# First-layer rows copied unscaled out of PSUM by ScalarE, leaky in SBUF by VectorE, six buffers for them, and a later schedule behind

## The chip, the cores and the metric

The kernel runs on one core of one Trainium2 chip. The metric is the device time of that core in microseconds, the median of several runs. The core has five engines, each with its own queue of instructions taken in order: TensorE (PE in the profile, its weight loads PEld), VectorE (DVE), ScalarE (ACT), GpSimd (POOL) and SyncE (SP, which issues most DMAs). They wait for one another by semaphores.

## The reference

A graph layer: 12500 nodes with 128 features, 412500 edges with 64 features, sorted by destination. For each edge, query, key and edge products go through a two-layer network with leaky ReLU (slope 0.2). Eight scores per edge are averaged, a softmax runs over all edges, and weighted value rows are summed per source node. Then come two normalisations.

```python
attn_in = jnp.concatenate([q[src], k[tgt], eh], axis=-1)
hmid = jax.nn.leaky_relu(attn_in @ A1 + b1, SLOPE)
scores = jax.nn.leaky_relu(hmid @ A2 + b2, SLOPE)
w = jax.nn.softmax(scores.mean(axis=-1), axis=0)
out = jax.ops.segment_sum(w[:, None] * v[tgt], src, num_segments=num_nodes)
y = h + out
```

`y` is normalised with `gamma` and `beta`, added to `x`, and normalised again.

## The kernel before

Two pipelines run side by side, each written as a generator or a list of steps, and interleaved in program order.

The first makes records. Edges come in 403 groups of 1024. For each group TensorE gathers key and value rows with one-hot matrices and adds the edge product (`rows`, L940 and L947) into banks of PSUM. ScalarE copies the banks to SBUF records (`evacuate`, L958 and L959; five buffers `rec`). GpSimd scatters every record to a table in HBM, sorted by block of source nodes (L970, 3224 indirect DMAs). VectorE works out the places (`onehots` L860 to L880, `masked` L910, `places` L921 and L923). A group takes six steps.

The second, `sums_of`, reads the table back in 250 units of up to 16 tiles of 128 rows (10 rounds of 25 units; units of two rounds have 12 tiles). A unit passes through these functions:

- `load` (L1154): one DMA into a buffer `rt`, six of which there are (two more in the last round). `sources` (L1199, L1201), `turned` and `put` (L1212, L1217), `spread` (L1222) and `load_q` (L1180) bring the source numbers and the queries to the partitions that need them; `onehot` (L1232) makes one-hot matrices of them.
- `hidden` (L1244, L1254): four times in a unit, four tiles each. TensorE adds the transposed key part and the query part in a bank of PSUM.
- `sloped` (L1265): ScalarE writes 0.2 times the bank into a buffer `hm` in SBUF. `leaky` (L1269): VectorE takes the maximum of bank and `hm`, back into `hm`.
- `scores` (L1280), `above_zero` (L1294), `heads` (L1306): the second layer, summed over heads.
- `maxima` (L1316, L1321): VectorE's score `S` and its maximum `mx` per partition; `maximum` (L1327): TensorE transposes `mx`; `reference` (L1336, L1337): VectorE's running reference `ref`; `weights` (L1346): ScalarE's exponentials `w`.
- `select` (L1355) and `weigh` (L1369): one-hot matrices of the nodes, times the weights. `add` (L1402): TensorE sums value rows. `before_it` (L1379) loads the sums of the round before into `old`, `lowered` (L1388, L1391) rescales, `total` (L1419, L1412) adds them, `store` (L1431) writes them.

Banks of PSUM come from one ring of five, `bank()`, which `rows`, `hidden` and `scores` share, so a new product waits until the bank of five before has been read. The buffers `hm` come from the pool `hp`, which has five.

What sets the order is the table that `lags` returns (L1109): for each function, how many steps behind the unit's own step `s0` it is issued. A new unit begins every 8 steps. `hidden` of piece k stands at `s0 + 2k`, and `onehot`, `sloped` and `leaky` count from there. A step's functions are issued in the order in which they were entered, those with `late=1` behind the others. A load stands no sooner than one step behind the last `add` of the unit that had its buffer (`load_at = mine[-held] + 1`), and at `s0 - 19` in all rounds but the last.

`closing` ends the kernel: it adds `beta` to `x` into a table (`rows_x`, `moved`, `put_x`), and then normalises 14 groups of seven blocks. It takes its buffers from pools opened late, in the space of the record pipeline.

Of the kernel before, what the change touches and what calls it, by code (L numbers as in the profile page):

```python
# [10 lines left out]
FP = mybir.dt.float32  # L11
# [4 lines left out]
AF = mybir.ActivationFunctionType  # L16
ALU = mybir.AluOpType
# [4 lines left out]
P = 128  # L22
D = 128
# [3 lines left out]
SLOPE = 0.2  # L27
NB = 7
# [3 lines left out]
MORE = 2  # L32
# [13 lines left out]
WR = 257  # L46
# [432 lines left out]
def sorted_path(  # L479
# [8 lines left out]
    nc = tc.nc  # L488
# [34 lines left out]
    for j, part in enumerate((1.0, -1.0)):  # L523
        nc.vector.tensor_scalar(
            A2s[:, H + 1 + j : H + 2 + j], A2s[:, H : H + 1], part * SLOPE / (1 - SLOPE), None,
            op0=ALU.mult,
# [6 lines left out]
    for j, part in enumerate((1.0, -1.0)):  # L533
        nc.vector.tensor_scalar(
            b2_r[:, H + 1 + j : H + 2 + j], b2_r[:, H : H + 1], part * SLOPE / (1 - SLOPE), None,
            op0=ALU.mult,
# [10 lines left out]
        out=signs, in_=signs, compare_op=ALU.not_equal, fill=SLOPE - 1, base=-(H + 2),  # L547
# [40 lines left out]
    TB = max(t for *_, t in plan.rounds)  # L588
    work = ctx.enter_context(ExitStack())
    pool = lambda name, bufs, **k: work.enter_context(tc.tile_pool(name=name, bufs=bufs, **k))  # L590
    hp = pool("hid", 5)
    Wqh, bias_qh, Wkv, bias_kv = (
        wts[:, 2 * D * i : 2 * D * (i + 1)].rearrange("k (s d) -> k s d", s=2)
        for wts in [hp.tile([D, 4 * P], FP, name="hm") for _ in range(2)] for i in range(2)
# [19 lines left out]
    with tc.tile_pool(name="prep", bufs=1) as prep, tc.tile_pool(  # L614
        name="pprep", bufs=1, space=PSUM
# [28 lines left out]
    blk = const.tile([P, T], BF)  # L644
# [79 lines left out]
    def spans():  # L724
# [21 lines left out]
    above = const.tile([P, P], BF)  # L746
    nc.gpsimd.memset(above, 1.0)
    nc.gpsimd.affine_select(
        out=above, in_=above, compare_op=ALU.is_gt, fill=0.0, base=0,
# [20 lines left out]
    late = {}  # L770
# [318 lines left out]
    for p, (*_, t) in enumerate(plan.rounds):  # L1089
        wide = max(1, min(BLK, WIDTH // t))  # L1090
# [11 lines left out]
    state = {}  # L1102
# [6 lines left out]
    def lags(p):  # L1109

        return dict(
            every=EVERY, lead=25 if p == NR - 1 else 19, sources=-13, turned=-12, spread=-7, q=-7,
            onehot=-2, sloped=2, leaky=3, scores=10, above=12, heads=13, maxima=15, maximum=15,
            reference=17, weights=18, old=13, lowered=21, select=16, weigh=18,
            add=(21, 22, 24, 25), total=27, store=30,
        )

    def sums_of(bp):


        plans, s0, free, starts, ends = [], 19, ([], []), {}, {}
        for p, bs, t in units:
            nt = len(bs) * t
            nk = -(-nt // 4)
            o = lags(p)
# [7 lines left out]
            s0 = max(s0, load_at + o["lead"] - 1)  # L1133
            if plans:
                s0 = max(s0, plans[-1][2] + EVERY)
# [9 lines left out]
        def do(step, fn, *args, late=0):  # L1145
            steps.setdefault(max(int(step // 1), 0), []).append((late + step % 1, fn, args))
# [113 lines left out]
            st["hm"][k] = hp.tile([D, 4 * P], FP, name="hm")  # L1260
            st["ph", k] = ph

        def sloped(i, t0, c, n, k):
            hm = state[i]["hm"][k][:, : n * P]
            nc.scalar.activation(hm, state[i]["ph", k][:, : n * P], AF.Copy, scale=SLOPE)  # L1265

        def leaky(i, t0, c, n, k):
            hm, ph = state[i]["hm"][k][:, : n * P], state[i].pop(("ph", k))
            nc.vector.tensor_tensor(hm, ph[:, : n * P], hm, op=ALU.max)  # L1269


        def slices(m):
# [166 lines left out]
        for i, (nt, nk, s0, load_at, o) in enumerate(plans):  # L1439
            do(load_at, load, i)  # L1440
            do(s0 + o["sources"], sources, i)
            do(s0 + o["turned"], turned, i)
            do(s0 + o["turned"], put, i)
            do(s0 + o["spread"], spread, i)
            do(s0 + o["q"], load_q, i)
            for k, (c, c1) in enumerate(pieces(i)):
                n, s = c1 - c, s0 + 2 * k
                t = units[i][2]
                for u in range(-(-c // t), (c1 - 1) // t + 1):
                    do(s + o["onehot"], onehot, i, u)  # L1450
                do(s, hidden, i, c, c, n, k)
                do(s + o["sloped"], sloped, i, c, c, n, k, late=1)
                do(s + o["leaky"], leaky, i, c, c, n, k, late=1)
            do(s0 + o["scores"], scores, i, 0, nt)
            do(s0 + o["above"], above_zero, i)
            do(s0 + o["heads"], heads, i, 0, nt)
            do(s0 + o["maxima"], maxima, i)
            do(s0 + o["maximum"], maximum, i, late=1)
            do(s0 + o["reference"], reference, i)
            do(s0 + o["weights"], weights, i)  # L1460
            do(s0 + o["old"], before_it, i)
            do(s0 + o["lowered"], lowered, i)
            for j, t0 in enumerate(range(0, nt, 4)):
                n = min(4, nt - t0)
                if t0 % SEL == 0:
                    m = min(SEL, nt - t0)
                    do(s0 + o["select"] + 2 * j, select, i, t0, m)
                do(s0 + o["weigh"] + 2 * j, weigh, i, t0, n)
                do(s0 + o["add"][j], add, i, t0, n)
            do(s0 + o["total"], total, i)  # L1470
            do(s0 + o["store"], store, i)
# [8 lines left out]
    def closing(bp, do, s0, s1, s2):  # L1480

        gb = {}

        def wide(b):
            return b.rearrange("p (o d) -> p o d", o=1).to_broadcast([P, NB, D])

        def three(b, k):
            return b[:, k * NB * D : (k + 1) * NB * D].rearrange("p (b d) -> p b d", d=D)

        def rows_x(g):  # L1490
            gb["x", g] = t = late["end"].tile([P, 2, 2, WR], FP, name="rec")
            t = t.rearrange("p a b w -> p (a b w)")
            nc.sync.dma_start(out=three(t, 0), in_=x[:, g * NB : (g + 1) * NB, :])
            nc.sync.dma_start(out=t[:, NB * D : NB * D + D], in_=beta.to_broadcast([P, D]))

        def moved(g):
            t = gb["x", g].rearrange("p a b w -> p (a b w)")
            nc.gpsimd.tensor_add(three(t, 0), three(t, 0), wide(t[:, NB * D : NB * D + D]))

        def put_x(g):  # L1500
            t = gb.pop(("x", g)).rearrange("p a b w -> p (a b w)")
            nc.sync.dma_start(out=xtab[:, g * NB : (g + 1) * NB, :], in_=three(t, 0))

        def load_gamma():
            gb["gamma"] = late["gamma"].tile([P, D], FP, name="gamma")
            nc.sync.dma_start(out=gb["gamma"], in_=gamma.to_broadcast([P, D]))

        for g in range(ng):
            do(s0 + 24 + 12 * g, rows_x, g)
            do(s0 + 30 + 12 * g, moved, g)  # L1510
            do(s0 + 34 + 12 * g, put_x, g)
        do(s0 + 30, load_gamma)


        def factors():
# [68 lines left out]
            st["y", k] = [parts[j // 4][:, j % 4 * D : (j % 4 + 1) * D] for j in range(NB)]  # L1584

        def diagonals(st):
            t = late["end"].tile([P, 2, 2, WR], FP, name="rec").rearrange("p a b w -> p (a b w)")
            st["dg"] = three(t, 0)
            nc.gpsimd.tensor_mul(
                st["dg"], wide(ident),  # L1590
                gb["facs"][:, st["bl"]].rearrange("p (b o) -> p b o", o=1)
                .to_broadcast([P, NB, D]),
            )
# [228 lines left out]
    with tc.manual_schedule():  # L1822
        n1, n3 = 6 * plan.rounds[0][1], 6 * G
        n0 = n1 * 9 // 10
        i1 = 6 * min(plan.gate, plan.rounds[0][1]) - 12
        pieces = list(fill(2))
        fills = [(i1 * j // len(pieces), piece) for j, piece in enumerate(pieces)]
        fills = sorted(fills, key=lambda piece: piece[0])[::-1]
        tabs, made, nt = tables(), 0, 1 + (2 * ng - 1) * (10 + 6) + ng
        more, sent, ne = later(), 0, 11 * (len(chunks) - 1)  # L1830
        done, r = 0, 0
        for i, _ in enumerate(_ for p in range(NP) for _ in make(p)):
            while fills and fills[-1][0] <= i:
                fill_piece(*fills.pop()[1])
            while made < nt and made * n0 < i * nt:
                next(tabs, None)
                made += 1
            while sent < ne and sent * n0 < i * ne:
                next(more, None)
                sent += 1  # L1840
            if i == n1:
                for _ in tabs:
                    pass
                for _ in more:
                    pass
                spans()
                covered()
                tab_pool.close()
                steps, starts = sums_of(pool("blk", BLKS))
            if i < n1:  # L1850
                continue
            while r + 1 < NR and i >= 6 * begun[r + 1]:
                r += 1
            if r + 1 < NR:
                until = starts[r] + (starts[r + 1] - starts[r]) * (i - 6 * begun[r]) / (
                    6 * (begun[r + 1] - begun[r])
                )
                while done < until:
                    for fn, args in steps[done]:
                        fn(*args)  # L1860
                    done += 1
        while done < starts[-1]:
            for fn, args in steps[done]:
                fn(*args)
            done += 1
        making.close()
        for name, of, bufs, k in (
            ("blk", "blk2", MORE, {}), ("end", "end", 4, {}), ("gamma", "gam", 1, {}),
            ("psm", "psm2", 1, dict(space=PSUM)),
        ):  # L1870
            late[name] = far(of, bufs, **k)
        for step in steps[done:]:
            for fn, args in step:
                fn(*args)
# [73 lines left out]
```

## Time and profile before

| | |
|---|---|
| runs | 5765.57 us median of 3, 5764.45 to 5776.47 |
| the profiled execution | 5754.63 us, its span 5752.9 us |
| mean granted TensorE clock | 0.833 |
| leaky, L1269 | 932 instructions, 631.7 us busy |
| scaled copy, L1265 | 932 instructions, 547.7 us busy |

The profile's page counts the busy time of each engine over the span and shows the span in 40 slices. Its groups of instructions give the line, the engine, the operation, its output and input by the program's names, the count, then the busy time in us and the mean of one in ns, and last the idle time of the engine just before them with what ended it. A wait is put down to the instruction that came last by the profile; "remote" stands for a releaser on none of the core's engines, "issue" for none that the profile shows. All durations are those of one execution.

### The profile page before, as it was taken

The numbers are of one execution on the slowest core, as the hardware profiler recorded it, in microseconds if no ns is written. First come the engines' busy times: TensorE is split into PE (matmuls) and PEld (weight loads), VectorE is DVE, ScalarE is ACT, GpSimd is POOL, SyncE is SP. The second block draws the span as 40 slices with busy tenths as digits, with TensorE's granted clock in tenths as the row PEclk, the third lists the DMA queues.
The fourth block names the chain that finished last, engine by engine and source line by source line (L and its number), as shares of the span: only waits on it lengthen the run. The fifth ranks groups of instructions, "written<-read, shape, count | busy, mean of one in ns | idle before, by whom it ended". The sixth has DMA issues, their size and how long they took to land. (4 is left out here: it accounts for less than half of the span.)

```text
span 5752.9 us, 91349 instructions
## 1 busy us (share of the span) xinstructions
PE 4343.1 (75%) x29928; PEld 3185.9 (55%) x29928; DVE 4003.1 (70%) x8452; ACT 3093.0 (54%) x8846; POOL 3315.0 (58%) x3279
## 2 busy tenths in 40 slices
PE   4546536777777877778778888887787888888887
PEld 2334324555555656555556655566665555556677
DVE  7778745666667677666666777767776766676677
ACT  2432224445555666555555665556555565556776
POOL 4776666666566655566665656555555556665103
PEclk7667657788888898888888898898888888888999
DMA  6888766766778888778788888888888887877975
GB/s 195 265 258 270 249 202 220 229 224 223 240 272 269 268 278 275 257 251 270 257 265 274 276 270 284 278 263 261 274 268 268 271 269 259 269 272 255 330 282 185
DMA packets 728991, 1487.94 MB, mean 259 GB/s; under 512 B 157584, under 2 KB 328227, under 8 KB 726710
## 3 DMA queue, kind: packets, MB, share of 16 engines
q1 hardware_dynamic: 537410, 1056.51, 57.7%
q0 software_dynamic: 154752, 424.43, 20.0%
q10 hardware_dynamic: 36340, 1.05, 0.4%
q8 instruction: 237, 3.88, 0.3%
q14 instruction: 252, 2.06, 0.1%
HBM read 902.30 MB, written 579.32 MB: 258 GB/s over the span
## 5 line engine op out<-in xcount | busy, mean ns | idle before, releaser
L970 POOL DMA_INDIRECT rtab<-rec,idx x3224 | 3230.3, 1002 | 2067.6 <-issue 830.3
L958 ACT ACTIVATE rec<-bank 128x512 f32<-128x512 f32 x1612 | 879.9, 595 | 1489.0 <-remote 653.1
L1402 PE MATMUL psm<-rt,ohw 128*128 128x128 f32 x7448 | 1226.2, 310 | 128.8 <-issue 126.1
L1369 ACT ACTIVATE ohw<-ohs,w 128x128 f32<-128x128 bf16 x3724 | 1214.2, 401 | 32.7 <-remote 8.5
L1402 PEld LDWEIGHTS psm<-rt,ohw 128*128 128x128 f32 x7448 | 1086.9, 218 | 214.0 <-issue 165.2
L1269 DVE TENSOR_TENSOR hm<-bank,hm 128x512 f32<-128x512 f32 x932 | 631.7, 678 | 390.2 <-ACT hm L1265 253.2
L940 PE MATMUL bank<-kvs,ohd 128*128 128x256 bf16 x3224 | 607.2, 309 | 366.7 <-ACT rec L958 255.8
L1244 PE MATMUL bank<-ident,rt 128*128 128x128 f32 x3724 | 681.2, 309 | 237.2 <-ACT z L1294 81.7
L1265 ACT ACTIVATE hm<-bank 128x512 f32<-128x512 f32 x932 | 547.7, 588 | 571.1 <-remote 214.6
L1244 PEld LDWEIGHTS bank<-ident,rt 128*128 128x128 f32 x3724 | 481.5, 158 | 524.2 <-issue 275.7
L947 PE MATMUL bank<-WeS,eat 64*128 64x128 f32 x6448 | 715.7, 340 | 48.3 <-issue 47.0
L947 PEld LDWEIGHTS bank<-WeS,eat 64*128 64x128 f32 x6448 | 524.6, 221 | 273.2 <-issue 269.7
L910 DVE TENSOR_TENSOR ats<-pc,oh 128x792 f32<-128x792 f32 x403 | 393.2, 976 | 389.6 <-remote 172.3
L1254 PE MATMUL bank<-ohT,qs 128*128 128x512 bf16 (+3 forms) x2156 | 639.8, 391 | 30.6 <-issue 29.3
L940 PEld LDWEIGHTS <-ohd 128*128 128x128 bf16 x3224 | 343.4, 112 | 573.0 <-issue 473.1
L1232 DVE TENSOR_SCALAR ohT<-rowB,iotaP,power 128x512 bf16<-128x512 uint8 (+1 forms) x980 | 563.9, 580 | 77.7 <-DMA rowB<-row 38.2
L880 DVE TENSOR_SCALAR ohd<-dstb,node 128x1152 bf16<-128x1152 uint8 x404 | 566.0, 1401 | 33.2 <-remote 25.2
L1355 DVE TENSOR_TENSOR ohs<-iotaE,sl 128x512 bf16<-128x512 bf16 x932 | 395.5, 424 | 3.2 <-ACT ohw L1369 2.8
L921 DVE TENSOR_REDUCE pos<-ats 128x8 f32<-128x792 f32 x403 | 390.5, 969 | 2.5
L1280 PE MATMUL bank<-hm,A2s 128*32 128x512 f32 x1864 | 353.6, 660 | 29.9 <-issue 25.4
L1419 DVE SCALAR_TENSOR_TENSOR old<-old,by,psm 128x512 f32<-128x512 f32 (+1 forms) x225 | 164.6, 732 | 215.2 <-remote 73.4
L1306 PEld LDWEIGHTS psS<-headsum,z 128*128 128x128 f32 (+2 forms) x2000 | 277.2, 212 | 30.9 <-issue 25.7
(199 smaller groups left out, 3815.1 us busy)
## 6 DMA issues: line engine op xcount, KB each, us to landing
rt<-rtab SPq DMA_DIRECT2D x192, 2056.0 KB
eat<-in_ea SPq DMA_DIRECT2D x201, 512.0 KB
rt<-rtab SPq DMA_DIRECT2D x48, 1542.0 KB
qs<-qtab SPq DMA_DIRECT2D x240, 256.0 KB
atab<-old SPq DMA_DIRECT2D x240, 256.0 KB
old<-atab SPq DMA_DIRECT2D x216, 256.0 KB
rtab<-rec,idx POOLq DMA_INDIRECT x3224
dstb<-dtab SPq DMA_DIRECT2D x201, 256.0 KB
```

The source lines that it names most:

```text
L880: nc.vector.tensor_scalar(to, row[:, cols], node, None, op0=ALU.is_equal)
L940: nc.tensor.matmul(pk[h][:, i, :], ohd[h * (GT // 2) + j + i], kvs, start=(i == 0), stop=False,)
L947: nc.tensor.matmul(pk[h][:, i, :D], eat[half, (j + i) * P : (j + i + 1) * P], WeS[half, :], start=False, stop=(i == 1),)
L958: nc.scalar.activation(rec[:, h, :, : 2 * D], pk[h], AF.Copy)
L970: one_tile = nc.gpsimd.indirect_dma_start(out=rtab[:, :], out_offset=bass.IndirectOffsetOnAxis(ap=idxs[g][:, t : t + 1], axis=0), in_=rec[ ...
L1232: nc.vector.tensor_scalar(st["oh"][u][:, : t * P].rearrange("p (t q e) -> p t q e", q=4, e=32), st["rowB"][:, : nt * P] .rearrange("p (q t ...
L1244: nc.tensor.matmul(ph[:, j * P : (j + 1) * P], st["rt"][:, t0 + j, :D], ident, is_transpose=True, start=(j == 0), stop=False,)
L1254: nc.tensor.matmul(ph[:, cols], st["qs"][:, u, s, :], st["oh"][u][:, (j0 - u * t) * P : (j1 - u * t) * P], start=False, stop=(s == 1 and j ...
L1265: nc.scalar.activation(hm, state[i]["ph", k][:, : n * P], AF.Copy, scale=SLOPE)
L1269: nc.vector.tensor_tensor(hm, ph[:, : n * P], hm, op=ALU.max)
L1369: nc.scalar.activation(ohw[:, j, :], ohs[:, :, t0 % SEL + j], AF.Copy, scale=st["w"][:, t0 + j : t0 + j + 1])
L1402: nc.tensor.matmul(st["psm"][:, u * P : (u + 1) * P], ohw[:, j, :], st["rt"][:, t0 + j, D : 2 * D], start=(k == 0), stop=(k == t - 1),)
```

## The change

ScalarE's step is now called `copied` and copies the bank without a scale, and it is the last reader of the bank. `leaky` reads and writes only `hm`: the maximum of `hm` times 0.2 and `hm`, one fused instruction on VectorE. The pool `hp` has six buffers. In the table, `leaky` stands two steps behind the copy instead of one; `scores`, `above` and `heads` two steps later than before, as are `maxima`; everything behind that, from `maximum` on, three steps later. To make room for the sixth buffer, the closing's tiles shrink from four times 257 to 896 columns, and `gamma` and `beta` are each loaded once into the space of the table `blk` of the record pipeline.

```diff
-    hp = pool("hid", 5)
+    hp = pool("hid", 6)
...
-            onehot=-2, sloped=2, leaky=3, scores=10, above=12, heads=13, maxima=15, maximum=15,
-            reference=17, weights=18, old=13, lowered=21, select=16, weigh=18,
-            add=(21, 22, 24, 25), total=27, store=30,
+            onehot=-2, copied=2, leaky=4, scores=12, above=14, heads=15, maxima=17, maximum=18,
+            reference=20, weights=21, old=16, lowered=24, select=19, weigh=21,
+            add=(24, 25, 27, 28), total=30, store=33,
...
-            nc.scalar.activation(hm, state[i]["ph", k][:, : n * P], AF.Copy, scale=SLOPE)
+            nc.scalar.activation(hm, state[i].pop(("ph", k))[:, : n * P], AF.Copy)
...
-            hm, ph = state[i]["hm"][k][:, : n * P], state[i].pop(("ph", k))
-            nc.vector.tensor_tensor(hm, ph[:, : n * P], hm, op=ALU.max)
+            hm = state[i]["hm"][k][:, : n * P]
+            nc.vector.scalar_tensor_tensor(hm, hm, SLOPE, hm, op0=ALU.mult, op1=ALU.max)
...
-            gb["x", g] = t = late["end"].tile([P, 2, 2, WR], FP, name="rec")
...
-            nc.sync.dma_start(out=t[:, NB * D : NB * D + D], in_=beta.to_broadcast([P, D]))
+            gb["x", g] = t = late["end"].tile([P, NB * D], FP, name="end")
...
+            gb["gamma"], gb["beta"] = (blk[:, 2 * D * i : 2 * D * (i + 1)].bitcast(FP) for i in range(2))
+            nc.sync.dma_start(out=gb["beta"], in_=beta.to_broadcast([P, D]))
```

On VectorE, in the middle of the program, around the maximum `mx` of one unit, the queue was:

```order
L1269 TENSOR_TENSOR hm<-bank,hm 128x512 [waits Activation_49]
L1355 TENSOR_TENSOR ohs<-iotaE,sl 128x512
L1232 TENSOR_SCALAR ohT<-rowB,iotaP,power 128x512 [waits DMAHW0_49,PE_49]
L1316 SCALAR_TENSOR_TENSOR S<-sl,psS 128x16 [waits PE_49]
L1321 TENSOR_REDUCE mx<-S 128x1 [waits DVE_49]
L1269 TENSOR_TENSOR hm<-bank,hm 128x512 [waits Activation_49]
```

At the same unit it is now (`Activation` in a wait is ScalarE, `DMAHW` a DMA):

```order
L1232 TENSOR_SCALAR ohT<-rowB,iotaP,power 128x512 [waits PE_49]
L1269 SCALAR_TENSOR_TENSOR hm<-hm 128x512 [waits Activation_49]
L910 TENSOR_TENSOR ats<-pc,oh 128x792 [waits PE_49]
L1355 TENSOR_TENSOR ohs<-iotaE,sl 128x512 [waits DVE_49,Activation_49]
L1316 SCALAR_TENSOR_TENSOR S<-sl,psS 128x16 [waits PE_49]
L1321 TENSOR_REDUCE mx<-S 128x1 [waits DVE_49]
```

The leaky has moved behind the next one-hot matrix (L1232) and no longer names a bank; it still waits for ScalarE. `select` (L1355) shows a wait for ScalarE of its own, which the leaky's wait covered before.

On SyncE, at the 136th load of `rt`, the queue of DMAs was:

```order
L1222 DMA rowB<-row 128x4x512 [waits DMAHW6_49,DMAHW2_49,DVE_49]
L1180 DMA qs<-qtab 128x1024 [waits DMAHW3_49,PE_49]
L1379 DMA old<-atab_72 128x512 [waits DMAHW7_49,DMAHW4_49]
L1154 DMA rt<-rtab 128x4x1028 [waits DMAHW5_49,PE_49]
L822 TENSOR_LOAD start
L827 ISA
L827 DMA kvs<-kvtab 128x256 [waits PE_49]
L847 DMA dstb<-dtab 128x2048 [waits DMAHW0_49,DVE_49]
L1431 DMA atab_73<-old 128x512 [waits DMAHW1_49,DVE_49]
```

It is now:

```order
L1222 DMA rowB<-row 128x4x512 [waits DMAHW3_49]
L1180 DMA qs<-qtab 128x1024 [waits DMAHW4_49,PE_49]
L1154 DMA rt<-rtab 128x4x1028 [waits DMAHW5_49,PE_49]
L822 TENSOR_LOAD start
L827 ISA
L827 DMA kvs<-kvtab 128x256 [waits DMAHW6_49]
L847 DMA dstb<-dtab 128x2048 [waits DMAHW7_49,DVE_49]
L1379 DMA old<-atab_72 128x512 [waits DMAHW1_49,DMAHW0_49]
```

The load of `rt` now stands ahead of the load of `old`, and its wait for TensorE (PE) is for the last `add` six units back, which has moved three steps towards it.

More of the change, by code (lines that the diff above doesn't have):

```diff
@@ L1261, in hidden, with copied @@
             st["ph", k] = ph
-        def sloped(i, t0, c, n, k):
+        def copied(i, t0, c, n, k):
             hm = state[i]["hm"][k][:, : n * P]
-            nc.scalar.activation(hm, state[i]["ph", k][:, : n * P], AF.Copy, scale=SLOPE)
+            nc.scalar.activation(hm, state[i].pop(("ph", k))[:, : n * P], AF.Copy)
         def leaky(i, t0, c, n, k):
-            hm, ph = state[i]["hm"][k][:, : n * P], state[i].pop(("ph", k))
-            nc.vector.tensor_tensor(hm, ph[:, : n * P], hm, op=ALU.max)
+            hm = state[i]["hm"][k][:, : n * P]
+            nc.vector.scalar_tensor_tensor(hm, hm, SLOPE, hm, op0=ALU.mult, op1=ALU.max)
         def slices(m):
@@ L1451, in sums_of @@
                 do(s, hidden, i, c, c, n, k)
-                do(s + o["sloped"], sloped, i, c, c, n, k, late=1)
+                do(s + o["copied"], copied, i, c, c, n, k, late=1)
                 do(s + o["leaky"], leaky, i, c, c, n, k, late=1)
@@ L1490, in rows_x, with load_ends @@
         def rows_x(g):
-            gb["x", g] = t = late["end"].tile([P, 2, 2, WR], FP, name="rec")
-            t = t.rearrange("p a b w -> p (a b w)")
+            gb["x", g] = t = late["end"].tile([P, NB * D], FP, name="end")
             nc.sync.dma_start(out=three(t, 0), in_=x[:, g * NB : (g + 1) * NB, :])
-            nc.sync.dma_start(out=t[:, NB * D : NB * D + D], in_=beta.to_broadcast([P, D]))
         def moved(g):
-            t = gb["x", g].rearrange("p a b w -> p (a b w)")
-            nc.gpsimd.tensor_add(three(t, 0), three(t, 0), wide(t[:, NB * D : NB * D + D]))
+            t = gb["x", g]
+            nc.gpsimd.tensor_add(three(t, 0), three(t, 0), wide(gb["beta"]))
         def put_x(g):
-            t = gb.pop(("x", g)).rearrange("p a b w -> p (a b w)")
+            t = gb.pop(("x", g))
             nc.sync.dma_start(out=xtab[:, g * NB : (g + 1) * NB, :], in_=three(t, 0))
-        def load_gamma():
-            gb["gamma"] = late["gamma"].tile([P, D], FP, name="gamma")
+        def load_ends():
+            gb["gamma"], gb["beta"] = (blk[:, 2 * D * i : 2 * D * (i + 1)].bitcast(FP) for i in range(2))
+            nc.sync.dma_start(out=gb["beta"], in_=beta.to_broadcast([P, D]))
             nc.sync.dma_start(out=gb["gamma"], in_=gamma.to_broadcast([P, D]))
+        do(s0 + 24, load_ends)
         for g in range(ng):
@@ L1511, in closing @@
             do(s0 + 34 + 12 * g, put_x, g)
-        do(s0 + 30, load_gamma)
         def factors():
@@ L1586, in diagonals @@
         def diagonals(st):
-            t = late["end"].tile([P, 2, 2, WR], FP, name="rec").rearrange("p a b w -> p (a b w)")
+            t = late["end"].tile([P, NB * D], FP, name="end")
             st["dg"] = three(t, 0)
@@ L1867, in sorted_path @@
         for name, of, bufs, k in (
-            ("blk", "blk2", MORE, {}), ("end", "end", 4, {}), ("gamma", "gam", 1, {}),
+            ("blk", "blk2", MORE, {}), ("end", "end", 4, {}),
             ("psm", "psm2", 1, dict(space=PSUM)),
```

## The prediction

> **What bounds the kernel now.** I read the page first (engine shares, then the 40 slices), then stretches of 600 us, then the waits, then the groups that keep shapes apart. The shares say that no engine is full:
>
> ```profile
> PE 4343.1 (75%) x29928; PEld 3185.9 (55%) x29928; DVE 4003.1 (70%) x8452; ACT 3093.0 (54%) x8846; POOL 3315.0 (58%) x3279
> PEclk7667657788888898888888898898888888888999
> 3000.00:3600.00 600.00, 494.95 (x3508) 359.69 (x3507) 427.18 (x911) 364.24 (x1070) 358.61 (x362) 0.88 0.84 278
> 4800.00:5400.00 600.00, 493.40 (x3386) 353.04 (x3382) 407.85 (x878) 360.13 (x1066) 314.64 (x312) 0.88 0.82 273
> ```
>
> The last two rows are stretches of the long middle, where records are made and rows are summed side by side: busy time of PE, PEld, DVE, ACT and POOL, then clock, DMA share and GB/s. PE is busy 495 of 600 us (82%), the DMA engines 84%, DVE 71%, ACT 61%. So PE and DMA stand nearest to full, and what is left is the engines waiting for each other. The chain that ended last is no help: it reaches back only over the last microseconds. Here are the waits that bear on the change:
>
> ```profile
> ACT rec L958 <- remote: 653.1, 150, 17.7
> PE bank L940 <- ACT rec L958: 255.8, 101, 13.6
> DVE hm L1269 <- ACT hm L1265: 253.2, 180, 5.4
> ACT w L1346 <- DVE ref L1337: 114.1, 61, 5.4
> PEld psS L1327 <- DVE mx L1321: 99.5, 54, 8.5
> PE psS L1327 <- DVE mx L1321: 78.9, 47, 7.9
> PE bank L1244 <- ACT rec L958: 61.7, 27, 5.6
> ```
>
> Columns: total us, times, longest. Three things are to be seen. VectorE stands 253 us before the leaky (L1269) because ScalarE's scaled copy (L1265), one step ahead of it, is not there. Behind VectorE, ScalarE waits 114 us for `ref`, and TensorE 79 us for `mx`, the maximum that it transposes at L1327. And what TensorE misses most, 256 + 62 us, are banks that ScalarE's record copies (L958) hold, while those copies wait 653 us for something on no engine ("remote").
>
> The bank that the leaky itself holds is a small item. From the answer on line L1269, who waited for it:
>
> ```profile
>   PE bank L940: 16.0, 6
>   PE bank L1244: 10.7, 10
> ```
>
> **The change part by part.** Durations, from the groups by form:
>
> ```profile
> L1269 DVE TENSOR_TENSOR hm<-bank,hm 128x512 f32<-128x512 f32 x930 | 630.8, 678 | 388.6 <-ACT hm L1265 253.2 <-issue 109.0 <-ACT ohw L1369 23.1
> L1728 DVE TENSOR_TENSOR less<-ns,sq 128x896 f32<-128x896 f32 x14 | 15.3, 1093 | 15.7 <-ACT sq L1723 13.5 <-issue 2.1
> L1728 DVE TENSOR_TENSOR less<-ns,sp 128x1792 f32<-128x1792 f32 x13 | 26.2, 2018 | 6.9 <-ACT sp L1723 5.9 <-issue 1.0
> L923 DVE SCALAR_TENSOR_TENSOR idx<-pos,twin 128x8 int32<-128x8 f32 x403 | 67.9, 168 | 13.8
> L1412 DVE COPY old<-psm 128x512 f32<-128x512 f32 x24 | 16.4, 685 | 27.2 <-remote 15.9 <-PE bank L947 4.5 <-PE bank L1280 2.6
> L1419 DVE SCALAR_TENSOR_TENSOR old<-old,by,psm 128x512 f32<-128x512 f32 x216 | 160.4, 742 | 215.2 <-remote 73.4 <-PE bank L947 45.4 <-PE psm L1402 44.8
> L1265 ACT ACTIVATE hm<-bank 128x512 f32<-128x512 f32 x930 | 546.9, 588 | 570.3 <-remote 214.6 <-PE bank L1254 92.8 <-PE bank L947 51.4
> L958 ACT ACTIVATE rec<-bank 128x512 f32<-128x512 f32 x1612 | 879.9, 595 | 1489.0 <-remote 653.1 <-issue 306.8 <-PE bank L947 200.7
> ```
>
> *The new leaky.* A fused multiply-and-max of 512 f32 elements within SBUF is in no row. Two-input operations in SBUF go from 1093 ns at 896 elements to 2018 at 1792, 1.032 ns an element; back to 512 that is 1093 - 384 x 1.032 = 697 ns. The small fused operation L923 (168 ns at 8) leads up to 168 + 504 x 1.032 = 688. Upper end: the fused form at L1419 stands 742 against 685 for a plain copy out of PSUM; 57 ns on top of 697 is 754. A gain is excluded, since these f32 rows pass about one element per ns, as L1269 does. I take 697, the row nearest in kind: +19 ns x 932 = 18 us of VectorE (9 to 71). VectorE idles 30% of the span, so I let half reach the end: +9 us.
>
> [...]
>
> *The copy without scale.* L958 is such a copy: 595 against 588 ns, 932 x 7 = 6.5 us of ScalarE, which is 54% busy; half is +3 (0 to 6.5).
>
> *The bank's release.* It now hangs on ScalarE's copy alone, one step sooner than the leaky's end. TensorE's 16.0 + 10.7 = 27 us go; next late there is the copy itself, whose place behind the product (two steps) stays.
>
> *Two steps between copy and leaky.* The period of a unit is its load's: first and last issue below, (5564.6 - 780.6) / 249 = 19.2 us, so a step (8 to a unit) is 2.40 us. The mean wait of the leaky is 253.2 / 180 = 1.4 us, the longest 5.4; one step more hides most of it. What stood behind the leaky in VectorE's queue comes sooner: `mx`, `ref`, `ats`. Besides, `maximum` goes one step behind `maxima` (18 against 17; both stood at 15), so that TensorE comes to `mx` 2.40 us later, against a mean wait of 78.9 / 47 = 1.7 us. I take all 79 us of that wait, and of ScalarE's 114 us for `ref` a third, 38, since `reference` to `weights` keeps its one step and only the delay that VectorE brought along goes.
>
> *Six hidden buffers, scores two steps later.* Scores of a unit now come before the third hidden product of the next one (step 12 = 8 + 4); four buffers and two of the next unit are six. Without the sixth, hidden products would wait two steps, 4.8 us a unit; with it nothing does.
>
> *Everything behind, three steps later.* The last `add` stands at 28 instead of 25, and the load of the unit six further on at 48 - 19 = 29. So the load follows the last reader of its buffer by one step instead of four. Its issue waits for that reader, and SyncE takes its queue in order. Here is what a load needs, and how it waits now (the issue row, its first consumer, then waits of that queue):
>
> ```profile
> L1154 SPq DMA_DIRECT2D rt<-rtab x250: 3/377/1304, 780.6 to 5564.6; - x125
> L1199 DVE CAST sl<-rt x125: 150/178/425, 790.1 to 4287.0; 128x32 bf16<-128x32 f32 x72, 128x12 bf16<-128x12 f32 x48, 128x8 bf16<-128x8 f32 x3, 128x6 bf16<-128x6 f32 x2
>   DMA rt<-rtab: 10.6, 1
> SPq L1154 <- PE bank L1280: 61.2, 17, 7.6
> SPq L1154 <- PE psm L1402: 53.4, 27, 4.9
> SPq L1222 <- DMA row<-slT: 420.5, 84, 9.4
> ```
>
> The first load was issued at 780.6 and read at 790.1 with VectorE waiting for it, so 9.5 us to land; it is the only one that VectorE waited for. From the release (step -20 seen from its own unit) to `sources` (step -13) there are now 7 steps, 16.8 us, where there were 10, 24.0. The margin over 9.5 us falls from 14.5 to 7.3 us: enough, if landing under load stays below 16.8. Queued behind a load on SP are the load of `old`, the next `kvs` and `dstb`, the store and the spread of `row` (L1222, which waits 420 us already). I charge 5 us, from 0 to 110 (below).
>
> *The closing.* `beta` is loaded once instead of 14 times, into a table that nobody reads any more. POOL's wait for it goes, but the only one who waited for that POOL work is POOL (L1498), and I count nothing. The queue of steps ends three later, which are steps without other work: 0, at most 3 x 2.40 = 7 us.
>
> ```profile
> rec<-in_beta SPq DMA_DIRECT2D x14, 64.0 KB
> POOL rec L1498 <- DMA rec<-in_beta: 160.4, 10, 40.8
>   POOL rec L1589: 58.8, 1
> ```
>
> *The sum.* Waits that go: 79 + 27 + 38 = 144 us. Not all of it shortens the span: PE is 82% busy, but DMA is 84% busy, and part of what PE gains it will wait again for record banks, whose 653 us "remote" the change doesn't touch. I choose half, 72 us, with none and all as bounds. Costs 9 + 3 + 5 = 17. So -55 us against the profiled execution's own 5754.6 (span 5752.9): 5700. The median of the runs lies 10.9 us above it (5765.57), so 5710.
>
> **The rivals.**
>
> *Nothing to be measured.* The waits move on to the record copies and to DMA: half becomes none, and costs of 17 at most. For it: DMA at 84% and 653 us of remote waits. Against it: PE's waits for `mx` are no DMA's. 5766, and 0.2% is 11.5 us here, about what a measurement can tell.
>
> *A larger gain.* PE sets the pace: all 144 go, and ScalarE, never held behind a late leaky, gives record banks back sooner, a quarter of 255.8 + 61.7 = 317.5, that is 79. 144 + 79 - 17 = 206: 5549, or 5560 beside the median. Against it: of the 1489 us that ScalarE idles before L958, 653 + 307 are put down to "remote" and "issue", not to anything that the change moves.
>
> *Loads too late (slower).* The load waits for the last `add` one step before it, and lands behind other transfers. It decides once landing takes over 16.8 us. At 17.8 each of the 219 units between the first 6 and the last 25 is 1 us late, and everything behind `sources` on VectorE with it: 219 us, half on the path, 110. 5754.6 - 72 + 12 + 110 + 10.9 = 5815. For it: 44 of the loads wait for L1280 or L1402 already with four steps between. Against it: one wait of VectorE for a load in 250.
>
> *VectorE and GpSimd hold each other (slower).* The leaky gets a second SBUF input, and GpSimd works 58% of the time on the scatters. What such pairs show now:
>
> ```profile
> L970 POOL DMA_INDIRECT rtab<-rec,idx x3224: 955/963/2778, 58.2 to 5300.2; - x190
> L1355 DVE TENSOR_TENSOR ohs<-iotaE,sl x932: 281/415/2215, 888.0 to 5615.2; 128x512 bf16<-128x512 bf16 x187
> ```
>
> L1355 reads two SBUF tiles, 415 ns in the median with a longest of 2215, so most are not held. If every leaky that meets a scatter waited for half of it, 932 x 0.58 x 0.48 = 260 us of VectorE, half on the path: 5710 + 130 = 5840. [...]
>
> **How the numbers follow.** Forecast (5710) 0.47; larger gain 0.15; nothing 0.15; loads late 0.17; held port 0.06. Faster by over 0.2% is the first two, 0.62; slower the last two, 0.23; same 0.15. The forecast's own range runs from all 144 (5638) to none (5754). For 8 in 10 the range goes down to 5605, which leaves out the lower half of the larger gain, and up to 5805, which leaves out the worst of the two slow cases.
>
> **What would show it.** Right: L1269 near 697 ns, its wait for L1265 below 60 us, PE's wait for `mx` below 30, no PE wait for L1269's bank, SP's wait at L1154 for L1402 up, and VectorE still not waiting for `rt`. Wrong: waits of L1199 or L1201 for `rt`, or of L1232 for `rowB`, in the tens of us (late loads); L1269 with a mean far over its median (the port); or `mx` waits gone with PE's waits for L958 grown by as much (nothing). A sum that failed by its share would show the three waits gone and the span lower by other than half of them.

## The result, and the profile after

The changed kernel takes 5672.4 us in the median of 4 runs (5657.5 to 5680.4), against 5766.4 us of the kernel before on the same chip: a ratio of 0.9839 [0.9808, 0.9869]. The forecast was 5710. The profiled execution of the changed kernel took 5666.2 us, 88 us less than that of before (5754.6). Here are its page's shares, the same two stretches as before, and the waits that answer to those of the prediction:

```profile
PE 4379.9 (77%) x29928; PEld 3200.3 (56%) x29928; DVE 3987.4 (70%) x8452; ACT 3097.1 (55%) x8846; POOL 3431.3 (61%) x3279
```

```profile
3000.00:3600.00 600.00, 508.43 (x3533) 370.87 (x3532) 434.54 (x918) 369.47 (x1084) 384.31 (x368) 0.87 0.83 280
4800.00:5400.00 600.00, 510.56 (x3596) 377.90 (x3595) 423.11 (x934) 387.81 (x1151) 307.92 (x284) 0.89 0.85 292
```

```profile
ACT rec L958 <- remote: 482.9, 136, 11.9
PE bank L940 <- ACT rec L958: 116.9, 48, 12.1
DVE hm L1269 <- ACT hm L1265: 6.8, 12, 0.9
ACT w L1346 <- DVE ref L1337: 9.1, 8, 1.6
PE psS L1306 <- ACT z L1294: 155.6, 88, 7.7
DVE m L1336 <- PE psm L1402: 122.4, 41, 8.2
```

The leaky's wait for the copy has gone (253.2 to 6.8 us), and with it ScalarE's wait for `ref` (114.1 to 9.1). TensorE misses the banks that ScalarE's record copies hold for 116.9 us at L940, where it was 255.8. Two waits are new: TensorE's for `z` at `heads` (L1306), 155.6 us, and VectorE's for TensorE ahead of `m` (L1336), 122.4 us where the view of before has 19.7. In the accounts of TensorE, its idle time fell from 5752.9 - 4343.1 = 1410 to 5664.4 - 4379.9 = 1285 us, and its busy time rose by 37: 125 - 37 = 88, the whole difference of the spans.

The groups of the same execution, with shapes kept apart (the idle time before them and its releasers at the end of each row):

```profile
L970 POOL DMA_INDIRECT rtab<-rec,idx x3224 | 3346.1, 1038 | 1896.5 <-issue 846.7 <-ACT rec L959 411.0 <-ACT w L1346 129.1
L1244 PE MATMUL bank<-ident,rt 128*128 128x128 f32 x3724 | 670.4, 303 | 68.9 <-issue 64.2 <-ACT rec L958 1.3 <-remote 1.0
L1269 DVE SCALAR_TENSOR_TENSOR hm<-hm 128x512 f32<-128x512 f32 x930 | 636.7, 685 | 9.5 <-ACT hm L1265 6.8 <-ACT rec L959 0.9 <-issue 0.3
L1327 PE MATMUL psS<-ident,mx 128*128 128x128 f32 x250 | 73.5, 294 | 5.1 <-issue 2.9 <-DVE mx L1321 0.6 <-DVE S L1316 0.6
```

The leaky takes 685 ns, 7 more than before; TensorE's wait for `mx` is 0.6 us (78.9), and its wait for record banks at L1244 is 1.3 (61.7). One row that no term of the sum has: GpSimd's scatter (L970) now takes 1038 ns in the mean. Its group in the kernel before, and that of L1244 there:

```profile
L1244 PE MATMUL bank<-ident,rt 128*128 128x128 f32 x3724 | 681.2, 309 | 237.2 <-ACT z L1294 81.7 <-issue 74.1 <-ACT rec L958 61.7
L970 POOL DMA_INDIRECT rtab<-rec,idx x3224 | 3230.3, 1002 | 2067.6 <-issue 830.3 <-ACT rec L959 603.4 <-ACT by L1388 186.7
```

So GpSimd has 116 us more to do. It also waits 192 us less for ScalarE's record (L959), and its last scatter starts at 5244.9 us where that of before started at 5300.2: here the longer scatters do not set the end. The row of L1244 shows that TensorE waited for `z` before, too, 81.7 us at this place; that wait has left it.

The loads of `rt`: SyncE's waits at L1154, and what VectorE's first reader (L1199) waited for, both of the changed kernel:

```profile
SPq L1154 <- PE psm L1402: 415.7, 65, 13.5
SPq L1154 <- PE bank L1280: 239.4, 36, 12.6
```

```profile
DVE sl L1199 <- DMA rt<-rtab: 11.9, 7, 3.6
```

SyncE now stands 415.7 us before a load until `add` is done, 65 times, and yet VectorE waits 11.9 us for a load, where it was 10.6. VectorE's wait for `rowB` at L1232, which the prediction had named as a sign of late loads, is 47.1 us; it was 38.2 before the change, so as a sign it could not tell.

### The profile page after: what moved, and what is told of

Its sections match the earlier page's. It is cut to its first block, busy times and chain, and to the rows that moved or that the text cites. A ratio compares the mean times of both kernels' runs of the same rounds, so it can differ in the third digit from the quotient of the medians.

```text
span 5664.4 us, 91119 instructions
## 1 busy us (share of the span) xinstructions
PE 4379.9 (77%) x29928; PEld 3200.3 (56%) x29928; DVE 3987.4 (70%) x8452; ACT 3097.1 (55%) x8846; POOL 3431.3 (61%) x3279
## 5 line engine op out<-in xcount | busy, mean ns | idle before, releaser
L970 POOL DMA_INDIRECT rtab<-rec,idx x3224 | 3346.1, 1038 | 1896.5 <-issue 846.7
L1402 PEld LDWEIGHTS psm<-rt,ohw 128*128 128x128 f32 x7448 | 1069.7, 216 | 243.5 <-issue 198.6
L1265 ACT ACTIVATE hm<-bank 128x512 f32<-128x512 f32 x932 | 550.0, 590 | 605.9 <-PE psm L1402 146.3
L947 PE MATMUL bank<-WeS,eat 64*128 64x128 f32 x6448 | 730.2, 333 | 109.2 <-issue 105.9
L940 PE MATMUL bank<-kvs,ohd 128*128 128x256 bf16 x3224 | 589.5, 303 | 259.8 <-ACT rec L958 116.9
L1244 PE MATMUL bank<-ident,rt 128*128 128x128 f32 x3724 | 670.4, 303 | 68.9 <-issue 64.2
L1232 DVE TENSOR_SCALAR ohT<-rowB,iotaP,power 128x512 bf16<-128x512 uint8 (+1 forms) x980 | 569.2, 584 | 160.2 <-remote 57.0
L1244 PEld LDWEIGHTS bank<-ident,rt 128*128 128x128 f32 x3724 | 473.2, 155 | 334.0 <-issue 227.8
L1269 DVE SCALAR_TENSOR_TENSOR hm<-hm 128x512 f32<-128x512 f32 x932 | 637.5, 684 | 9.5 <-ACT hm L1265 6.8
L940 PEld LDWEIGHTS <-ohd 128*128 128x128 bf16 x3224 | 335.1, 110 | 442.0 <-issue 345.5
L1306 PE MATMUL psS<-headsum,z 128*128 128x4 f32 (+2 forms) x2000 | 304.4, 274 | 165.2 <-ACT z L1294 155.6
L1306 PEld LDWEIGHTS psS<-headsum,z 128*128 128x128 f32 (+2 forms) x2000 | 297.8, 224 | 224.3 <-ACT z L1294 199.4
L1355 DVE TENSOR_TENSOR ohs<-iotaE,sl 128x512 bf16<-128x512 bf16 x932 | 394.0, 423 | 36.5 <-ACT ohw L1369 32.8
L1280 PE MATMUL bank<-hm,A2s 128*32 128x512 f32 x1864 | 377.7, 664 | 42.7 <-issue 32.7
```

The source lines that it names most:

```text
L940: nc.tensor.matmul(pk[h][:, i, :], ohd[h * (GT // 2) + j + i], kvs, start=(i == 0), stop=False,)
L947: nc.tensor.matmul(pk[h][:, i, :D], eat[half, (j + i) * P : (j + i + 1) * P], WeS[half, :], start=False, stop=(i == 1),)
L970: one_tile = nc.gpsimd.indirect_dma_start(out=rtab[:, :], out_offset=bass.IndirectOffsetOnAxis(ap=idxs[g][:, t : t + 1], axis=0), in_=rec[ ...
L1232: nc.vector.tensor_scalar(st["oh"][u][:, : t * P].rearrange("p (t q e) -> p t q e", q=4, e=32), st["rowB"][:, : nt * P] .rearrange("p (q t ...
L1244: nc.tensor.matmul(ph[:, j * P : (j + 1) * P], st["rt"][:, t0 + j, :D], ident, is_transpose=True, start=(j == 0), stop=False,)
L1269: nc.vector.scalar_tensor_tensor(hm, hm, SLOPE, hm, op0=ALU.mult, op1=ALU.max)
```

## The experiments

The kernels ran on three more chips. The kernel before takes 5859.5 us on the first of them, but 4869.3 and 4865.3 on the other two. Every ratio below is to the kernel before on the same chip, so ratios and not times are compared across chips; edits are shown against the changed kernel.

### Form or table: four kernels on the chip with 5859.5 us

The changed table and six buffers with the old leaky, one step behind the scaled copy:

```diff
-            onehot=-2, copied=2, leaky=4, scores=12, above=14, heads=15, maxima=17, maximum=18,
+            onehot=-2, copied=2, leaky=3, scores=12, above=14, heads=15, maxima=17, maximum=18,
...
+            nc.scalar.activation(hm, state[i]["ph", k][:, : n * P], AF.Copy, scale=SLOPE)
...
+            nc.vector.tensor_tensor(hm, ph[:, : n * P], hm, op=ALU.max)
```

> The changed kernel's table and six buffers, but the leaky as before: ScalarE writes 0.2 times the bank, VectorE takes the maximum of bank and buffer one step later (leaky 3). Theory A (the distances in the table make the gain; where the leaky reads from is a side matter): near the changed kernel, 5675 to 5705, with TensorE's wait for mx still under 10 us; VectorE's wait for L1265 is back at 150 to 250 us, and TensorE's waits for the leaky's bank at 10 to 40 us. Theory B (the bank's early release makes it): most of the gain is lost, 5735 to 5765. On the scatters (the longer mean of L970, 1038 ns against 1002): if the second SBUF input of the leaky holds GpSimd, the mean is back near 1002 ns here; if the closer schedule does it, it stays near 1038.

Measured: 5823.7 us, 0.9929 [0.9903, 0.9955]. That lies between the two theories, and L970 is back at 999 ns. VectorE's wait for L1265 is 282.0 us, TensorE's for `mx` 1.3.

The new form alone, everything else as before (five buffers, the old table and closing):

```diff
+            onehot=-2, sloped=2, leaky=3, scores=10, above=12, heads=13, maxima=15, maximum=15,
+            reference=17, weights=18, old=13, lowered=21, select=16, weigh=18,
+            add=(21, 22, 24, 25), total=27, store=30,
```

> The kernel before, its table and its five buffers, with nothing but the new form: an unscaled copy, and the leaky in SBUF one step behind it. Theory A: little, 5740 to 5770, with the wait for mx still 60 to 100 us and VectorE's for L1265 at 200 to 300 us. Theory B: most of the gain, 5670 to 5710. The mean of L970 should rise to 1030 or more if the second SBUF input holds GpSimd; otherwise it stays at 1002.

Measured: 5815.4 us, 0.9921 [0.9897, 0.9945], between the two theories again. L970 takes 1023 ns, more than with the old form and less than the 1030 that was expected.

The changed kernel, with `maximum` in the step of `maxima`:

```diff
-            onehot=-2, copied=2, leaky=4, scores=12, above=14, heads=15, maxima=17, maximum=18,
+            onehot=-2, copied=2, leaky=4, scores=12, above=14, heads=15, maxima=17, maximum=17,
```

> The changed kernel with maximum at 17, the step of maxima, as both stood in one step before; all else as changed. Theory A, if the extra step is what took TensorE's wait for mx away: the wait is back at 50 to 90 us and the time rises by half of that, 5695 to 5720. Rival: the wait went because VectorE no longer stands before the leaky; then it stays below 20 us and the time stays within 10 us of the changed kernel.

Measured: 5768.9 us, 0.9834 [0.9807, 0.9861], the gain of the whole change (0.9839 on the chip of the result): the rival holds. The changed kernel itself did not run on this chip.

The changed kernel, with `leaky` one step behind the copy:

```diff
-            onehot=-2, copied=2, leaky=4, scores=12, above=14, heads=15, maxima=17, maximum=18,
+            onehot=-2, copied=2, leaky=3, scores=12, above=14, heads=15, maxima=17, maximum=18,
```

> The changed kernel with leaky at 3, one step behind the copy as before; all else as changed. Theory A, if VectorE's standing before the leaky costs time: its wait for L1265 is back at 150 to 250 us and the time rises by 20 to 40, 5690 to 5715. Rival: that wait hid behind others; it comes back and the time stays within 10 us of the changed kernel.

Measured: 5788.4 us, 0.9873 [0.9843, 0.9903]. VectorE's wait for L1265 is back at 221.5 us.

Form and table bring about 0.8% and 0.7%, and their product, 0.985, lies between the two kernels that have both (0.9834 and 0.9873). The wait for `mx`, on which the largest term of my sum stood, in the waits of the new form alone and then of the kernel with `maximum` in the same step:

```profile
PE psS L1327 <- DVE mx L1321: 100.2, 46, 10.1
```

```profile
PE bank L940 <- ACT rec L958: 96.8, 45, 9.2
PE psS L1306 <- ACT z L1294: 132.9, 82, 6.3
PE psS L1327 <- DVE mx L1321: 13.1, 15, 1.4
DVE hm L1269 <- ACT hm L1265: 10.8, 17, 1.5
```

Without `maximum`'s extra step the wait for `mx` is still down to 13.1 us, and the time is as good. In the kernel with that step and the leaky one step behind the copy it is 0.8 us. Either slack does. Whether the extra step between copy and leaky pays by itself is not shown: without it the ratio is 0.9873, and its interval overlaps those of 0.9834 and 0.9839, so it is worth a few tenths of a per cent at most.

The new form alone is the run that bears most on the sum. The waits for `mx` (100.2 us), of the leaky for the copy (291.3) and of ScalarE for `ref` (115.2) are no smaller than those that the kernel before has on the chip of the result, and still it gains 44 us. So about half of the gain does not come from those waits.

### Late loads, late scores: four kernels on the chip with 4869.3 us

The changed kernel itself again, and three edits of one number pair each:

```diff
+            onehot=-2, copied=2, leaky=4, scores=12, above=14, heads=16, maxima=18, maximum=18,
...
+            onehot=-2, copied=2, leaky=4, scores=11, above=13, heads=15, maxima=17, maximum=18,
...
+            every=EVERY, lead=25 if p == NR - 1 else 17, sources=-13, turned=-12, spread=-7, q=-7,
```

The changed kernel:

> The changed kernel itself, beside the others of this job. Every theory: about 0.984 of the kernel before, with the mean of L970 at 1038 ns.

Measured: 4902.3 us, 1.0073 [1.0056, 1.0091]. On this chip the change makes the kernel slower, where every theory had 0.984. L970 takes 1046 ns.

`heads` and `maxima` one step later:

> The changed kernel with heads at 16, maxima at 18 and maximum at 18: one step more between z and heads, none between maxima and maximum. Theory A (the wait for mx only moved forward in TensorE's queue, to the wait for z before heads, 156 us, which costs as the other did): the wait for z falls to 60 us or less, and the time by 20 to 50 us against the changed kernel. Rival (the waits for z hide TensorE's next work, which would wait anyway): the time stays within 12 us.

Measured: 4889.9 us, 1.0040 [1.0024, 1.0056]. TensorE's wait for `z` at L1306 falls from 103.2 us to 2.8, and the time by 12, at the edge of what the rival allows; its wait for `mx` rises from 20.2 us to 31.9.

`scores` and `above` one step sooner:

> The changed kernel with scores at 11 and above at 13: z one step sooner, heads stay at 15. Theory A: TensorE's wait for z falls to 60 us or less and the time by 20 to 50 us. Rival: scores now stand one step behind the last leaky of the unit, so that TensorE waits for hm at L1280 instead, 50 us or more, and nothing is won.

Measured: 4899.9 us, 1.0066 [1.0050, 1.0082], no change. Neither sign came: the wait for `z` is 92.5 us, that for `hm` at L1280 2.9.

The load two steps later:

> The changed kernel with all loads but the last round's two steps later (lead 17 for 19), so 5 steps between load and sources instead of at most 7. If the margin behind the loads is as used up as the queue's waits say (SyncE waits some 1500 us at L1154), each of 219 units loses up to two steps of 2.4 us less what margin is left: VectorE's waits for rt come to 200 to 700 us and the time rises by 100 to 350. If a margin of 5 us or more is left, the time stays within 15 us and those waits below 50.

Measured: 4922.6 us, 1.0121 [1.0100, 1.0142], 20 us more than the changed kernel, while VectorE's waits for `rt` go from 174.0 us to 184.4: between the two expectations. A load that comes two whole steps later costs only 20 us, so what the change delays the loads by can hardly be most of the 33 us that it loses here.

### Loads or GpSimd: four kernels on the chip with 4865.3 us

Two theories were left for the loss: the later loads (L), and a GpSimd held by the new leaky (H). The kernel before was profiled here, with the form alone and the old form in the new table (both as above), and the new form in a table that is later by one step instead of three:

```diff
+            onehot=-2, copied=2, leaky=4, scores=11, above=13, heads=14, maxima=16, maximum=16,
+            reference=18, weights=19, old=14, lowered=22, select=17, weigh=19,
+            add=(22, 23, 25, 26), total=28, store=31,
```

The kernel before:

> The kernel before, unchanged, for a profile on the chip of this job. Where waits put down to issue and remote are few, as in the changed kernel's profile at 4904 us (PE issue 4 us in total), the time is near 4870; where they are many, near 5770 to 5860.

One run, 4874.9 us. VectorE already waits 85.4 + 107.8 us for loads of `rt` here, against 97.5 + 76.5 in the changed kernel on the chip like it: those waits are no doing of the change.

The form alone:

> The kernel before with the new form alone, as in e2, whose loads keep their four steps behind the last add. On a chip with few waits of issue and remote. Theory L (the later schedule costs there, since loads of rt come too late): no slower than before, ratio 0.985 to 1.000, VectorE's waits for rt below 50 us. Theory H (the leaky's second SBUF input costs there, since it holds GpSimd): ratio 1.003 to 1.010. On a chip with many such waits both expect 0.992 again.

Measured: 4918.8 us, 1.0111 [1.0096, 1.0126], just above the range of H; VectorE's waits for `rt` are 163.4 us.

The old form in the new table:

> The changed kernel's table and buffers with the old form of the leaky, as in e1. On a chip with few waits of issue and remote. Theory L: slower than before, 1.005 to 1.012, VectorE's waits for rt 100 us or more. Theory H: 0.990 to 1.000, with L970 back at 1000 ns. On a chip with many such waits both expect 0.993 again.

Measured: 4820.5 us, 0.9906 [0.9892, 0.9921]: faster than both kernels on such a chip, in the range of H, though VectorE's waits for `rt` are 218.8 us.

The new form in the table that is later by one:

> A version made of what stood out: the new form, leaky two steps behind the copy, six buffers, but everything from scores on only one step later than before (maxima 16 and maximum 16, last add 26), so the load keeps three steps behind it. On a chip with few waits of issue and remote. Theory L: 0.985 to 1.000, waits for rt below 50 us. Theory H: 1.003 to 1.010. On a chip with many such waits both expect 0.980 to 0.992.

Measured: 4872.2 us, 1.0017 [1.0008, 1.0026], between the two ranges; the waits for `rt` are 97.0 us, and L970 takes 1045 ns.

L is refuted as the main cause: the form alone loads as before did, and loses 1.1%; the old form has the late loads, and gains 0.9%. The rows for H are those of the scatter: from the answers on line L970 its minimum, median and longest, its first and last start, and the idle time up to "issue"; and the groups. First the kernel before on this chip:

```profile
L970 POOL DMA_INDIRECT rtab<-rec,idx x3224: 954/960/2787, 59.2 to 4418.3; - x190
  issue: 773.8, 2534
```

```profile
L970 POOL DMA_INDIRECT rtab<-rec,idx x3224 | 3230.6, 1002 | 1185.4 <-issue 773.8 <-ACT rec L959 99.4 <-DMA rtab<-rec,idx 62.7
L958 ACT ACTIVATE rec<-bank 128x512 f32<-128x512 f32 x1612 | 870.6, 593 | 1000.4 <-DMA rtab<-rec,idx 666.2 <-PE bank L947 272.4 <-issue 22.9
```

The idle time put down to "issue" is no slack: 773.8 / 2534 = 0.305 us, and in the two profiles of the result no gap between two scatters is under 0.303. So 3224 scatters take 3224 x (1.002 + 0.305) = 4214 us, of the 4359 in which they run: GpSimd is 97% full. On the chip of the result the same sum gives 3224 x (1.002 + 0.309) = 4227 of 5242 us, 81%. Now the form alone, the same views:

```profile
L970 POOL DMA_INDIRECT rtab<-rec,idx x3224: 954/960/2793, 59.1 to 4462.5; - x190
  issue: 793.6, 2594
```

```profile
L970 POOL DMA_INDIRECT rtab<-rec,idx x3224 | 3347.7, 1038 | 1112.6 <-issue 793.6 <-DVE both L870 59.8 <-DMA rtab<-rec,idx 55.2
L958 ACT ACTIVATE rec<-bank 128x512 f32<-128x512 f32 x1612 | 871.2, 594 | 1085.1 <-DMA rtab<-rec,idx 767.0 <-PE bank L947 231.2 <-issue 22.2
```

The scatters need 3224 x (1.038 + 0.306) = 4333 us and run for 4403, 44 us longer than before; ScalarE waits 101 us more for a record buffer that is still being scattered. Of all groups L970 is the only one whose busy time grew by over 26 us; it grew by 117. And the old form in the new table:

```profile
L970 POOL DMA_INDIRECT rtab<-rec,idx x3224: 954/960/2792, 59.4 to 4381.7; - x190
```

```profile
L970 POOL DMA_INDIRECT rtab<-rec,idx x3224 | 3228.5, 1001 | 1151.0 <-issue 776.6 <-ACT rec L959 86.2 <-DVE both L870 59.2
```

Here 1001 ns, and the stage is done in 4322 us, less than the 4333 that GpSimd alone needs with the new form. With scatters of 1038 ns this time can't be reached, whatever the table.

Why the scatters take longer is to be seen in the time line of the form alone (start, duration, engine), first GpSimd, then VectorE's leakies of the same microseconds:

```profile
2532.88 1.03 POOL L970 DMA_INDIRECT rtab<-rec,idx  x1 [0.30 <-issue]
2534.22 1.40 POOL L970 DMA_INDIRECT rtab<-rec,idx  x1 [0.30 <-DVE ref L1337]
2535.93 0.96 POOL L970 DMA_INDIRECT rtab<-rec,idx  x1 [0.30 <-issue]
2537.19 1.33 POOL L970 DMA_INDIRECT rtab<-rec,idx  x1 [0.30 <-issue]
```

```profile
2532.30 0.68 DVE L1269 SCALAR_TENSOR_TENSOR hm<-hm 128x512 f32<-128x512 f32 x1
...
2534.11 0.68 DVE L1269 SCALAR_TENSOR_TENSOR hm<-hm 128x512 f32<-128x512 f32 x1
...
2537.04 0.65 DVE L1269 SCALAR_TENSOR_TENSOR hm<-hm 128x512 f32<-128x512 f32 x1
```

The second scatter lies beside a leaky for 2534.79 - 2534.22 = 0.57 us and takes 0.44 longer than the median; the fourth beside one for 0.50, 0.37 longer; the first for 0.10, 0.07 longer; the third beside no leaky, 0.96. In the records of the two profiles of the result, 244 scatters of over 1.3 us lie beside a leaky, where before 9 did.

All three that are longer start while a leaky is at work, and that decides. In the changed kernel's profile of the result, 233 scatters start with over 0.2 us of a leaky still to come; in the median they are longer by that overlap less 0.13 us. Of 462 that were under way when a leaky began, the median is longer by 0.00 us. With the old form, 165 scatters start beside a leaky in the same way, and their median is not longer either. All 398 scatters that start beside a leaky are together 123 us longer than 0.96 us each; with the old form 293 are, by 8. The difference is the 116 us by which the group has grown.

## Why the prediction was right, and where it was not

*The direction and the size.* Faster, as forecast, by 88 us in the profiles and 94 in the medians, where I had 55.

*The waits that go.* All three went: `mx` 79 to 0.6 us, the leaky's bank 27 to none, ScalarE's for `ref` by 105 where I took 38. "Besides, `maximum` goes one step behind `maxima` ... I take all 79 us" holds in its sum, but its reason isn't needed: the leaky's slack alone leaves 13 us. And it was not a net gain, for TensorE now waits 156 us for `z` at L1306, where it had waited 82 us for `z` at L1244, though `heads` stands one step behind `above` as it did. On the chip with 4869 us, taking that wait away was worth 12 us.

*The bank's release and the share of one half.* This is where the sum failed in size. I gave the new form 27 us of TensorE's waits for the leaky's bank, half of them to be won, against 9 + 3 us of costs: about nothing. By itself it gained 44 us on the chip with 5859.5 us, and there the other waits of the sum stayed. And I argued that part of what TensorE gains "it will wait again for record banks, whose 653 us "remote" the change doesn't touch". The record banks did the contrary: TensorE's waits for them fell from 255.8 + 61.7 = 317 to 118 us, and the remote wait itself from 653 to 483. That is the mechanism of the rival with the larger gain, which I had given a quarter of the 317; it was nearly two thirds (199 us), while the new waits for `z` and ahead of `m` took a part back; so 88 lies between the forecast's 55 and the rival's 206. That ScalarE, freed of a leaky that holds its copies up, returns the banks sooner fits these rows; no run tests it by itself. It fits too that with the new form alone the waits for record banks are 166.0 + 5.9 = 172 us, but the kernel before was not profiled on that chip. The upper end of the forecast's own range was added up wrongly: with none of the waits gone and 17 us of costs it is 5782, not 5754.

*The new leaky.* I took 697 ns; it is 685, against the 678 of the old form.

*Loads too late.* Refuted on the result's chip (11.9 us of wait at L1199), and as the main cause of the loss on the others. The margin of 7.3 us sufficed, though SyncE waits long for `add`.

*VectorE and GpSimd hold each other.* I gave it 0.06, with "so most are not held", from L1355 and its bf16 tiles, and with VectorE as the one that is held. What the runs show is the reverse: in the changed kernel's profile of the result the leaky takes 684 ns beside a scatter and 685 without one, and it is the scatter that is longer, in the time line above by 0.44 us where 0.57 us of a leaky was still to come.

My reading of the trace was wrong, since I looked at VectorE's rows for a wait that lies in the scatter's. The scatter of 2778 ns that my row of L970 gives as the longest starts beside L1728, the very operation from which I priced the new leaky. In the kernel before:

```profile
297.35 2.78 POOL L970 DMA_INDIRECT rtab<-rec,idx  x1 [0.30 <-issue]
```

```profile
297.28 2.01 DVE L1728 TENSOR_TENSOR less<-ns,sp 128x1792 f32<-128x1792 f32 x1
```

It lies beside it for 299.29 - 297.35 = 1.94 us and is longer by 1.82. Of the 26 scatters that start beside an L1728 of 1792 elements, the median is longer by the overlap less 0.12 us. Beside L1355 they are longer as well: in the changed kernel, 36 scatters start with over 0.15 us of it to come and no other TENSOR_TENSOR or SCALAR_TENSOR_TENSOR beside them, and the median is longer by the overlap less 0.13 us, mostly too little to stand out.

On the result's chip the longer scatters cost little, as far as the shares tell: GpSimd was 81% full and is 84% full now. On the two quick chips it is nearly full, 97% with the kernel before on one and, by 3224 x (1.046 + 0.306) of 4420 us, 99% with the changed kernel on the other. There the form turns the gain of the table (0.9906 on the first) into a loss (1.0073 for the whole change on the second).

*Open.* Why the chips differ by 900 us and more was not found. The granted clock is 0.83 against 0.89, and on the quick chips the waits of ScalarE's record copies are named after the scatters' DMAs (666 us) where the slow one has 653 us of "remote"; the two may be the same wait. The DMA engines show 0.99 busy there in the stretch from 3000 to 3600 us, with and without the new form, so GpSimd isn't the only resource near its end. Not tried: a leaky with one input in SBUF at the changed table's distance.

## What to carry to other kernels

A buffer that one engine returns sooner can pay in the waits of a third one: here TensorE's waits for record banks fell by 199 us, more than all the waits that the sum had counted; that this made the gain was not tested by itself. Before an operand is moved from PSUM to SBUF, price the change on the other engines too: here VectorE's leaky went from 678 to 685 ns, and GpSimd's scatter, which the change doesn't touch, from 1002 to 1038. Look for it in an engine's longest instructions, and in what ran beside them when they began. A gain of 1.6% on one chip was a loss of 0.7% on another with the same program; read which engine is full there before carrying it over.

## What the runs showed of the hardware that was not expected

- The kernel before takes 5766, 5860, 4869 and 4865 us on four runs' chips, at granted clocks of about 0.83 on the first two and 0.89 on the last two.
- A scatter's instruction on GpSimd (0.96 us in the median) that starts while VectorE works on the new leaky, on L1728 (both f32) or on L1355 (bf16), each with two inputs in SBUF, is longer in the median by the overlap less 0.12 to 0.13 us (233, 26 and 36 scatters). One already under way when the new leaky begins is not longer in the median (462 scatters), nor is one that starts beside the old leaky, with one input in PSUM (165). The new leaky takes 684 ns beside a scatter and 685 without one. That two inputs are what decides is not shown: beside L1232, with one wide input, 209 scatters of the kernel before start with over 0.2 us of it to come, and their median is longer by the overlap less 0.13 us as well.
- Between two scatters GpSimd lies idle for 0.303 us at least in the two profiles of the result, and what the profile calls "issue" there is 0.305 to 0.313 us in the mean in each of the 14 profiles: by 1.002 of 1.307 us, the 3224 scatters would be back to back at 77% busy.
